# Second half chunk's normalisation two scan slots later, its store one slot later, in groups 1 to 3 of a scan-and-attention kernel

## The chip, the cores and the metric

The kernel runs on one core of one Trainium2 chip. The metric is the device time of one launch in microseconds (us). The figure before is the median of three runs.

## The reference, cut to what matters

The input is 32 sequences of 256 tokens with 256 features, in float32. Each sequence passes through one state-space layer (Mamba-like, with an added conditioning vector), then through two layers of local attention (window 128, 8 heads of 64) and gated feed-forward (hidden size 682), each with its residual. The input is added to the result. In outline, with the layer's names:

```python
xr, gate = split(x @ W_in.T)                # 512 channels each
xc = silu(causal_conv4(xr + cond) + b_conv)
xn = layernorm(xc) * ln_g + ln_b            # over the 512 channels
Bm, Cm, dt = split(xn @ W_xproj.T)          # 16 states each, for each token
Ad = 1 - 0.01 * tanh(dt @ W_dt.T + b_dt) * tanh(A_log)
Bd = Bm * minimum(norm(xn), 1.0)            # the row length of xn, at most 1
for t in range(256):                        # the recurrence; h is (16, 512) for a sequence
    h = clip(h * Ad[t] + Bd[t] * xn[t], -10, 10)
    y[t] = sum(Cm[t] * h)
u = (y + D * xn) * silu(gate) @ W_out.T
for layer in range(2):
    u = u + local_attention(rotary(l2norm(q)), rotary(l2norm(k)), v) @ wo
    u = u + (a * gelu(g)) @ w2 + b2         # a, g from the layernormed u
return x + u
```

So each token's normalised row xn is needed three times: for the figures Bm, Cm, Ad of its token (its length among them), as the input of the recurrence, and in the skip product with D.

## The kernel before, in words

**Tiling.** The sequences are taken in four groups of 8 (`GB`). A group's recurrence runs over 256 steps, in 8 chunks of 32 tokens (`CH`), so there are 32 chunks in all; they are numbered 0 to 31 here, 8 to a group. The state h of a group is one tile of 128 partitions (8 sequences by 16 states) by 512 channels, and one step of the recurrence is one VectorE (DVE) instruction, L716. A chunk has 256 rows (8 sequences by 32 tokens); its layer normalisation is done on two half chunks j = 0 and 1 of 128 rows each (`NJ` = 2).

**Stages.** The scan of group 0 runs alone at first. The scans of groups 1 to 3 then run beside the attention and feed-forward of the groups before them, sequence by sequence (64 units of a sequence and a layer). The attention and feed-forward of the last group end the kernel with no scan beside them.

**What sets the order.** Inside `group_scan`, `at(slot, what, ...)` enters each piece of scan work in a numbered slot; a slot is one step of the recurrence, and the chunk's first step has the number s0. `scan_slots` merges the groups' slots, and the main loop at the end of `program` emits scan slots between the stages of attention and feed-forward. The order of emission is not the final order: a scheduler in the compiler's front end, with costs of its own, takes it as a priority and settles the order of instructions on each engine and the use of the eight PSUM banks. Only a few instructions are pinned with `keep_in_program_order`. Each engine then runs its own instructions in that settled order, and waits at the head of its queue for semaphores.

**The normalisation of half chunk j of a chunk**, with slots counted from s = s0 - 26 + 4j:

- `norm_turn` (slot s): TensorE (PE) transposes xc into a PSUM bank called tp_x.
- `norm_stats` (s + 2): DVE takes mean and variance (L558, L560, L562, L567), and GpSimd (POOL) raises the variance to the power -1/2 (L565).
- `norm_shift` and `norm_apply` (s + 5): ScalarE (ACT) makes the shift (L572) and writes xn from tp_x with scale and shift (L579), which frees the bank.
- `norm_affine` (s + 6): POOL multiplies by the layer's scale and adds its offset (L586, L587).
- `norm_out` (s + 9): SP stores xn in device memory, in xnd (L591), and ACT squares xn with a running sum into ss (L593). The square's own output, sq_x, lies in a ring of two buffers, "th", which the conv's tanh (L504) and the gate's tanh (L768) use too.

**What follows from it.** `length` (slot s0 - 11): DVE clips the sums of squares (L599) and POOL takes the root (L600). `figures` and `figures_in` build each token's figures (DVE L609, PE L618, DVE L630 to L636), and `decays` the decay factors (ACT L643, DVE L648 to L656, POOL L660, L661; L669 makes the read-out matrix ly from them). SP reads each row of xnd back, spread over the 16 states (xrep, L685, slot s0 + t - 6), ACT scales it with beta (L706, s0 + t - 2), and DVE makes the step (L716, s0 + t). PE reads the state out (y, L728), and z is formed (L758 skip product on POOL, L773 gate product and L779, L799 on DVE).

**Other lines that are spoken of.** The conv of the next chunk: L469 and L483 (POOL, start and carry of the conv window), L472 (DVE, conditioning added), L478 (POOL) and L489 (DVE), the taps, L504 (ACT, tanh), L509 (DVE). Projections of later groups are made ahead and loaded with L447; gate inputs are loaded with L455. The attention: L989 (PE, qkv), L1002 (ACT, squares), L1005 to L1019 (DVE) and L1013, L1021, L1022 (POOL, rotary and norm), L1028 (PE, transposes), L1033 (ACT, copies qT and kT), L1215 (PE, scores), L1227 (ACT, exponentials), L1252 and L1271 (PE, row sums and values ov), L1260 (DVE, rinv), L1278 (ACT, oT), L1039 (PE, output). The feed-forward: L1353 (ACT, hT), L1375 (PE, pa), L1386 (ACT, gate ag), L1393 (DVE, gate product ag), L1402 (PE, po_f), L1413 (DVE, residual).

Of the kernel before, what the change touches and what calls it, by code (L numbers as in the profile page):

```python
# [73 lines left out]
def kernel(  # L74
# [147 lines left out]
    def program(ctx, exact):  # L222
# [154 lines left out]
        def group_scan(g):  # L377
# [8 lines left out]
            alone = g == 0  # L386
# [5 lines left out]
            def at(s, what, *args):  # L392
                agendas[-1].setdefault(s, []).append(partial(what, *args))
# [462 lines left out]
            for c in range(NCH):  # L856
                s0 = c * CH
                for hb in range(CH // TB):
                    s = s0 + hb * TB
                    for i in range(NI):  # L860
                        at(s + 4 * i + 5, read_out, c, hb, i)
                    at(s + 21, gated, c, hb)
                    at(s + 25, out_gate, c, hb)
                    at(s + 11, skip, c, hb)
                for ch in range(NC_):
                    at(s0 - 38 + 2 * ch, conv_in, c, ch)
                    at(s0 - 37 + 2 * ch, conv_taps, c, ch)
                    at(s0 - 36 + 2 * ch, conv_th, c, ch)
                    if not alone:
                        at(s0 - 35 + 2 * ch, conv_out, c, ch)  # L870
                for ch, s in enumerate((13, 16, 17, 18)):
                    at(s0 + s + 2, gate_th, c, ch)
                    if not alone:
                        at(s0 + s + 4, gate_out, c, ch)
                at(s0 - 25, raw_copy, c)
                at(s0 - 24, raw_turn, c)
                for j in range(NJ):
                    s = s0 - 26 + 4 * j
                    at(s + 2, norm_stats, c, j)
                    at(s + 5, norm_shift, c, j)  # L880
                    at(s + 5, norm_apply, c, j)
                    at(s + 6, norm_affine, c, j)
                    at(s + 9, norm_out, c, j)
                at(s0 - 11, length, c)
                at(s0 - 9, figures, c)
                at(s0 - 7, figures_in, c)
                at(s0 - 6, decay_th, c)
                at(s0 - 5, decays, c)
                at(s0 - 4, put_c, c, 0)
                at(s0 + 4, put_c, c, 1)  # L890
                for d in range(KM):
                    at(s0 + 45 + 2 * d, copy_y, c, d)
                    at(s0 + 46 + 2 * d, put_y, c, d)
            agendas.append({})
            for c in range(NCH):
# [20 lines left out]
                for hb in range(CH // TB):  # L916
                    s = s0 + hb * TB
# [5 lines left out]
            if alone:  # L923
                n = (NG - 1) * NCH * 2
                for u in range(n):
                    s = -30 + u * (NCH * CH) // n
# [6 lines left out]
        def scan_slots(groups):  # L933


            slots, scans = {}, [group_scan(g) for g in groups]
            for part in range(2):
                for i, agendas in enumerate(scans):
                    for s, what in agendas[part].items():
                        slots.setdefault(i * S + s, []).extend(what)  # L940
            for s in range(min(slots), max(slots) + 1):
                for what in slots.get(s, ()):
                    what()
                yield s
# [717 lines left out]
```

## Time and profile before

| what | value |
|---|---|
| time, median of 3 runs | 3586.82 us (3584.0 to 3589.47) |
| time of the profiled execution | 3582.75 us |
| its span | 3581.0 us |
| mean granted clock | 0.992 |
| PE busy | 3446.0 us, 96% |
| DVE busy | 2667.3 us, 74% |
| ACT busy | 1998.7 us, 56% |
| POOL busy | 1892.2 us, 53% |
| chain that ended last | PE 61%, DVE 19%, DMA 7%, POOL 6%, ACT 4%, issue 3% |
| row scaling L706, 960 times | mean 718 ns |
| recurrence step L716, 1024 times | mean 938 ns |
| gate product L1393, 320 times | mean 474 ns |

The profile records one execution. In lists of waits each line names the engine and instruction that waited, what it waited for, the total, the number of times and the longest. In a timeline each line has start, duration, engine, line, operation, output and input, and in square brackets the engine's idle time just before it with what ended it. Busy time of an engine that is not the latest costs nothing; a wait of PE, which is busy 96% of the span, is the first thing to look for. A chunk of the later groups takes two units, some 103 us (the one followed most closely runs from about 1700 to 1803 us), so one slot is about 3.2 us.

### The profile page before, as it was taken

The numbers are of one execution on the slowest core, as the hardware profiler recorded it, in microseconds if no ns is written. First come the engines' busy times: TensorE is split into PE (matmuls) and PEld (weight loads), VectorE is DVE, ScalarE is ACT, GpSimd is POOL, SyncE is SP. The second block draws the span as 40 slices with busy tenths as digits, with TensorE's granted clock in tenths as the row PEclk, the third lists the DMA queues.
The fourth block names the chain that finished last, engine by engine and source line by source line (L and its number), as shares of the span: only waits on it lengthen the run. The fifth ranks groups of instructions, "written<-read, shape, count | busy, mean of one in ns | idle before, by whom it ended". The sixth has DMA issues, their size and how long they took to land.

```text
span 3581.0 us, 57673 instructions
## 1 busy us (share of the span) xinstructions
PE 3446.0 (96%) x20220; PEld 2253.9 (63%) x20220; DVE 2667.3 (74%) x5049; ACT 1998.7 (56%) x3599; POOL 1892.2 (53%) x1842
## 2 busy tenths in 40 slices
PE   7999989999999999999999999999999999999999
PEld 4555335666656666666666666666666677777777
DVE  5888889888788777888787778888877555555553
ACT  4666656656555665566566655655666444434442
POOL 4433477645556555655565556555544454544551
PEclk9999999999999999999999999999999999999999
DMA  7887665445354545444454555534454112011101
GB/s 207 219 221 213 198 174 149 120 117 143 109 144 125 149 141 148 130 118 127 118 142 125 138 149 140 143 106 131 114 141 122 54 50 61 13 30 38 33 27 37
DMA packets 468767, 435.68 MB, mean 122 GB/s; under 512 B 228723, under 2 KB 308084, under 8 KB 468340
## 3 DMA queue, kind: packets, MB, share of 16 engines
q1 hardware_dynamic: 384018, 419.88, 42.0%
q10 hardware_dynamic: 84450, 12.01, 2.0%
q8 instruction: 163, 2.67, 0.3%
q14 instruction: 136, 1.11, 0.1%
HBM read 383.54 MB, written 46.66 MB: 120 GB/s over the span
## 4 chain that ended last, share of the span: by engine, by line
PE 61%; DVE 19%; DMA 7%; POOL 6%; ACT 4%; issue 3%; SPq 0%; ACTq 0%; DVEq 0%; POOLq 0%
PE ps_qkv L989 13%; PE pa L1375 13%; DVE h L716 7%; PE po_f L1402 7%; DMA xrep<-xnd 5%; PE ps_wo L1039 5%; PE y L728 4%; PE ov L1271 4%; PE sc L1215 3%; PE ps_out L808 3%; PE ps_in L399 2%; PE tr_qk L1028 2%; PE rs L1252 2%; ACT xrep L706 2%; DVE acc L489 2%
## 5 line engine op out<-in xcount | busy, mean ns | idle before, releaser
L716 DVE CUSTOM_DVE_ANT_0 h<-h,xrep,lim 128x512 f32<-128x512 f32 x1024 | 961.0, 938 | 228.9 <-ACT xrep L706 196.6
L706 ACT ACTIVATE xrep<-xrep,beta 128x512 f32<-128x512 f32 x960 | 672.3, 718 | 341.4 <-DMA xrep<-xnd 219.8
L989 PE MATMUL ps_qkv<-qkv,res 128*128 128x512 f32 x1536 | 713.5, 601 | 17.9 <-DVE rinv L1260 8.4
L1375 PE MATMUL pa<-hT,w 128*128 128x256 f32 (+1 forms) x2816 | 675.1, 382 | 11.3 <-DVE zT L799 10.7
L1375 PEld LDWEIGHTS pa<-hT,w 128*128 128x128 f32 (+1 forms) x2816 | 516.9, 188 | 152.9 <-issue 35.4
L1013 POOL TENSOR_TENSOR rot<-rot,swp 128x512 f32<-128x512 f32 x256 | 339.9, 1328 | 475.3 <-DVE swp L1010 423.5
L1021 POOL TENSOR_TENSOR rn<-ss,neg_half 128x8 f32<-128x8 f32 x256 | 466.8, 1823 | 18.4 <-DVE ss L1019 7.8
L989 PEld LDWEIGHTS ps_qkv<-qkv,res 128*128 128x128 f32 x1536 | 282.2, 191 | 301.6 <-issue 241.4
L728 PE MATMUL y<-h,ly 128*32 128x512 f32 x2048 | 348.9, 609 | 16.9 <-DVE h L716 13.9
L1327 POOL TENSOR_TENSOR rstd<-ve,neg_half 128x2 f32<-128x2 f32 x64 | 46.9, 733 | 527.6 <-DVE ve L1325 511.3
L1393 DVE SCALAR_TENSOR_TENSOR ag<-pa,b_sb,ag 128x256 f32<-128x256 f32 x320 | 151.6, 474 | 222.4 <-ACT ag L1386 222.3
L1402 PE MATMUL po_f<-ag,w 128*128 128x256 f32 x1280 | 309.0, 389 | 5.9 <-DVE fo L1413 3.8
L1022 POOL TENSOR_TENSOR rot<-rot,rn 128x512 f32<-128x512 f32 x256 | 289.4, 1130 | 20.0
L1402 PEld LDWEIGHTS po_f<-ag,w 128*128 128x128 f32 x1280 | 236.8, 191 | 71.3 <-issue 12.0
L1386 ACT ACTIVATE ag<-pa,b_sb 128x256 f32<-128x256 f32 x320 | 150.2, 469 | 233.1 <-PE pa L1375 232.1
L1002 ACT ACTIVATE sq<-ps_qkv 128x512 f32<-128x512 f32 x256 | 150.8, 595 | 185.1 <-PE ps_qkv L989 119.4
L1039 PE MATMUL ps_wo<-oT,wo 128*128 128x256 f32 x1024 | 231.7, 379 | 0.5 <-DVE ag L1393 0.5
L489 DVE SCALAR_TENSOR_TENSOR acc<-xr,wc_sb,acc 128x256 f32<-128x256 f32 x384 | 195.1, 531 | 47.7 <-POOL acc L478 47.2
L1005 DVE TENSOR_TENSOR rot<-ps_qkv,rc_sb 128x512 f32<-128x512 f32 x256 | 174.8, 683 | 65.6 <-ACT sq L1002 65.0
L1039 PEld LDWEIGHTS ps_wo<-oT,wo 128*128 128x128 f32 x1024 | 194.4, 190 | 28.1 <-DVE ag L1393 0.9
L1227 ACT ACTIVATE pT<-sc 128x512 f32<-128x512 f32 x384 | 202.3, 603 | 7.6 <-PE sc L1215 5.8
L1271 PE MATMUL ov<-pT,v_sb 128*64 128x256 f32 (+1 forms) x2048 | 183.7, 330 | 19.4 <-DVE ag L1393 19.3
(160 smaller groups left out, 5482.8 us busy)
## 6 DMA issues: line engine op xcount, KB each, us to landing
xrep<-xnd SPq DMA_DIRECT2D x960, 256.0 KB
rb<-inv SPq DMA_DIRECT2D x128, 256.0 KB
xnd<-xn SPq DMA_DIRECT2D x64, 256.0 KB
qkv<-in_wqkv_dram SPq DMA_DIRECT2D x24, 512.0 KB
ahead<-xs_a SPq DMA_DIRECT2D x48, 256.0 KB
xp<-ahead SPq DMA_DIRECT2D x48, 256.0 KB
xd<-xnd SPq DMA_DIRECT2D x192, 64.0 KB
w<-in_w_dram SPq DMA_DIRECT2D x80, 128.0 KB
```

The source lines that it names most:

```text
L489: nc.vector.scalar_tensor_tensor(acc, xr[:, :, k : k + CH], wc_sb[:, ch, k : k + 1], acc, ALU.mult, ALU.add,)
L706: scaled = nc.scalar.activation(bx, ck[c].pop(("bx", t), bx), AF.Copy, scale=ck[c]["beta"][:, t : t + 1])
L716: nc.vector._custom_dve(TENSOR_ADD_SAT, out=h_new, in0=state["h"], in1=bx, s0=ck[c]["lim"][:, 0, t : t + 1], s1=ck[c]["lim"][:, 1, t : t + 1],
L728: nc.tensor.matmul(ck[c]["y", hb][32 * q : 32 * q + 32, :], ly[hb % 2][:, 32 * t : 32 * t + 32], ck[c].pop(("h", hb * TB + t)), start=(i = ...
L989: nc.tensor.matmul(ps, res[b][:, k, t0 : t0 + W], wt["qkv", a][:, k], start=(k == 0), stop=(k == KM - 1),)
L1013: nc.gpsimd.tensor_add(rot, rot, swp)
L1021: nc.gpsimd.tensor_tensor(rn, ss, neg_half, ALU.pow)
L1022: nc.gpsimd.tensor_mul(rot, rot, bc(rn, 2, DH))
L1039: nc.tensor.matmul(po[:, d], wt["wo", 0][:, c, d * P : (d + 1) * P], oT[:, c, :], start=(c == 0), stop=(c == NC_ - 1),)
L1271: nc.tensor.matmul(ov[r * DH : (r + 1) * DH, i, kw * W :], self.qkv[b][2][:, kw, h * DH : (h + 1) * DH], self.p.pop((b, kw, i0 + i, r)), s ...
L1375: nc.tensor.matmul(dst[x], wt["w1", m][:, k, x], self.h[:, k], start=(k == 0), stop=(k == KM - 1),)
L1402: nc.tensor.matmul(self.po[:, d], wt["w2", 0][:, m, d * P : (d + 1) * P], self.ag[m], start=(m == 0), stop=(m == len(MCH) - 1),)
```

## The change

For the second half chunk (j = 1), and only in groups 1 to 3 (`not alone`), shift, apply and the affine step are entered two slots later, and the store with the square one slot later. The first half chunk and group 0 keep their slots. It concerns 24 chunks. No instruction is added, removed or resized. As the changed kernel has one more line, its lines past 880 are numbered one higher than before.

```diff
@@ -877,10 +877,11 @@
                 for j in range(NJ):
                     s = s0 - 26 + 4 * j
                     at(s + 2, norm_stats, c, j)
-                    at(s + 5, norm_shift, c, j)
-                    at(s + 5, norm_apply, c, j)
-                    at(s + 6, norm_affine, c, j)
-                    at(s + 9, norm_out, c, j)
+                    late = 2 if j and not alone else 0
+                    at(s + 5 + late, norm_shift, c, j)
+                    at(s + 5 + late, norm_apply, c, j)
+                    at(s + 6 + late, norm_affine, c, j)
+                    at(s + 9 + late // 2, norm_out, c, j)
                 at(s0 - 11, length, c)
                 at(s0 - 9, figures, c)
                 at(s0 - 7, figures_in, c)
```

## The prediction, made before the changed kernel ran

> **What bounds the kernel now.** I read the stages first. Columns: stretch, its length, then busy us and instruction count of PE, PE's weight loads, DVE, ACT and POOL, then clock and DMA.
>
> ```profile
> 500.00:1400.00 900.00, 858.61 (x5272) 551.09 (x5271) 744.43 (x1389) 541.83 (x988) 522.99 (x501) 0.99 0.48 134
> 1400.00:2700.00 1300.00, 1267.76 (x7907) 842.69 (x7906) 1038.53 (x1974) 782.56 (x1423) 747.14 (x694) 1.00 0.48 131
> 2700.00:3581.00 881.00, 873.17 (x5192) 632.43 (x5191) 471.21 (x921) 375.55 (x643) 400.98 (x332) 1.00 0.16 45
> ```
>
> The changed chunks 8 to 31 lie almost wholly in the first two stretches. There PE is idle for 900 - 858.61 = 41.4 us and 1300 - 1267.76 = 32.2 us. A reordering of other engines can earn only what PE waits: at most 73.6 us, 2.1%, and less if a wait moves. Next, PE's waits in 1400 to 2700 (total, times, longest):
>
> ```profile
> PE ov L1271 <- DVE ag L1393: 15.0, 11, 1.4
> PE ps_qkv L989 <- DVE rinv L1260: 7.1, 12, 0.9
> PE pa L1375 <- DVE zT L799: 6.5, 5, 1.9
> ```
>
> All are on DVE; none is on a normalisation step. ACT's waits from 500 to 2700 tell another story:
>
> ```profile
> ACT stat L572 <- POOL stat L565: 144.9, 40, 8.3
> ```
>
> This looks like the change's target: the shift L572 reaches the head of ACT's queue long before POOL has made its power. The steady chunk around 1700 to 1803 shows why (start, us, engine, operation; idle before it in brackets):
>
> ```profile
> 1716.00 0.47 ACT L1386 ACTIVATE ag<-pa,b_sb 128x256 f32<-128x256 f32 x1 [1.61 <-PE pa L1375]
> 1723.16 0.29 ACT L572 ACTIVATE stat<-nm,stat 128x1 f32<-128x1 f32 x1 [6.69 <-POOL stat L565]
> 1723.49 0.78 ACT L579 ACTIVATE xn<-tp_x,stat 128x512 f32<-128x512 f32 x1
> 1724.17 0.71 ACT L706 ACTIVATE xrep<-xrep,beta 128x512 f32<-128x512 f32 x1
> 1724.78 0.57 ACT L1033 COPY qT<-tr_qk 128x512 f32<-128x512 f32 x1
> 1725.24 0.59 ACT L1033 COPY kT<-tr_qk 128x512 f32<-128x512 f32 x1
> ```
>
> ```profile
> 1717.28 2.09 POOL L1021 TENSOR_TENSOR rn<-ss,neg_half 128x8 f32<-128x8 f32 x1
> 1719.45 1.04 POOL L1022 TENSOR_TENSOR rot<-rot,rn 128x512 f32<-128x512 f32 x1
> 1720.45 1.72 POOL L758 TENSOR_TENSOR xd<-xd,dskip_sb 128x512 f32<-128x512 f32 x1
> 1722.13 0.99 POOL L565 TENSOR_TENSOR stat<-ve,neg_half 128x1 f32<-128x1 f32 x1
> ```
>
> POOL's power stands behind the rotary work and the skip product, so ACT idles 6.69 us. Yet from 1700 to 1752 PE is busy 52.00 of 52.00 us: this stall costs PE nothing. PE waits only later in the chunk, when DVE, almost without a break from 1752 on (26.70 of 28 us up to 1780), is late with its gate product:
>
> ```profile
> 1764.78 0.43 DVE L472 TENSOR_TENSOR xr<-xp,cond_sb 128x256 f32<-128x256 f32 x1
> 1777.61 0.45 DVE L1393 SCALAR_TENSOR_TENSOR ag<-pa,b_sb,ag 128x256 f32<-128x256 f32 x1
> ```
>
> ```profile
> 1778.21 1.52 PE L1271 MATMUL ov<-pT,v_sb 128*64 128x256 f32 x16 [1.37 <-DVE ag L1393]
> ```
>
> **What the Trainium skill says.** "Perfetto Trace Analysis", Sequencer Loop: an engine instruction is put in its engine's queue and waits there for its semaphores. The trace agrees: ACT executed nothing in the 6.69 us although later work was ready. "SBUF — State Buffer", Who interferes with whom: a DVE instruction with two SBUF inputs contends with a GpSimd instruction that reads SBUF. This bears on the scale and offset L586, L587 if they meet other DVE work; the trace has L586 between 1.28 and 1.73 us, in keeping with that, but doesn't show the cause. "ScalarE: Activation LUTs", Rules for kernel authors, asks 2.7 us per switch of table set; here a load takes 1.28 us, so the trace's figure is used.
>
> **The change part by part.** Nothing is added or removed, ACT's 126 table loads included. Slots only set priorities, so I compared the two built programs engine by engine. PE's order is the same throughout.
>
> *Shift and apply (L572, L579), two slots later.* In 22 of 24 chunks L572 keeps the same predecessors in ACT's queue. In the steady chunks (18 to 31) it still stands directly behind the L1386 of 1716.00, and POOL's L565 behind the same rotary work. **The 6.69 us stall stays.** What moves is the next row scaling L706, now behind the copies qT and kT: 1725.72 - 1724.78 = 0.94 us later. A step L716 on DVE is then 0.94 us later, before 1752, where DVE has 52 - 39.28 = 12.7 us of idle time and another L706 is issued some 6 us earlier than now. Value 0; bound without that cover 14 x 0.94 = 13 us, below nothing the 0.94 us that qT and kT come sooner, which PE, busy throughout, can't use: 0. As L579 keeps its place, it frees PSUM bank tp_x no later: 0 in 22 chunks. In chunks 8 and 9 L572 goes behind one or two more row scalings, 0.6 to 1.3 us. The chain through L600 to L609 has about 5 us in hand there by the trace: 0, bounded at -2 to +2 us.
>
> *Scale and offset (L586, L587), two slots later.* They depend on L579 and stay behind it on POOL: 0. If they meet more two-input DVE work, the trace's own spread, 1.73 - 1.28 = 0.45 us, bounds it at ±0.45 us a chunk, hidden before 1752.
>
> *Store and square (L591, L593), one slot later.* On SP the store's first reader is the row load six slots before the chunk's first step; the store moves from 13 slots ahead to 12, leaving 6 slots of about 3.2 us, 19 us: 0. SP also splits or delays gate loads by 4 to 6 row loads; they are used about 50 us later: 0. On ACT the square changes place with the fourth gate tanh in the ring of two "th" buffers, so it now waits for the third gate product L773 (ends 1748.47), and goes behind the four exponentials, to about 1749.8 + 0.6 = 1750.4. The length L599 waits for it on DVE, with the scan step and the convolution queued behind it. Now:
>
> ```profile
> 1744.73 0.61 ACT L593 ACTIVATE sq_x<-xn 128x512 bf16<-128x512 f32 x1
> ```
>
> ```profile
> 1749.12 0.15 DVE L599 TENSOR_SCALAR ss<-ss 128x2 f32<-128x2 f32 x1
> 1751.06 0.81 DVE L716 CUSTOM_DVE_ANT_0 h<-h,xrep,lim 128x512 f32<-128x512 f32 x1 [1.46 <-ACT xrep L706]
> ```
>
> DVE waits for a row until 1751.06 anyway, so 1750.4 is hidden with 0.66 us to spare: 0. Bound: none below, since an earlier finish isn't possible; above, the square's own 0.61 + 0.19 = 0.8 us a chunk.
>
> *What the planner moved along.* In 12 chunks (18 to 29) one L472 goes from ahead of the late L1393 to behind beta (L654). It occupies 1765.12 - 1764.78 = 0.34 us of DVE's queue. PE's wait of 1.37 us behind L1393 shrinks by as much: 12 x 0.34 = **-4.1 us**. It isn't lost at the next wait: before rinv (L1260) DVE idles 2.06 us for an ACT operation that follows PE's own earlier matmuls, and L472 fits there. Only L472's carry copy waits for it on POOL, behind ly (L669). Bounds 0 and -4.1. In chunks 8 to 17 the order is irregular and a few exchanges go either way: value 0, bounded by a fifth of that stretch's 41.4 us, ±8 us.
>
> *Sum.* Profiled execution 3582.75 us (3581.0 span and 1.75 around it) - 4.1 = 3578.65. It lies 4.07 us below the median of the runs, 3586.82; the same step from there gives **3582.7 us**.
>
> **The rivals.**
> *A: it does what it says.* The shift gives way, if only in the irregular chunks, and PE's waits there that come through ACT or the scan disappear: in 500 to 1400 these are y on h 6.9, ps_out on xn 2.8, ps_st on hT 2.8, sc on pT 2.3, tr_qk on oT 1.9 and ps_qkv on oT 1.3, together 18.0 us. For it: one ACT stall, 8.3 us, is followed by a PE wait of 2.8 us on xn. Against: queue positions. 3586.8 - 18.0 = 3568.8.
> *B: slower, the square.* It ends more than 0.66 us later than worked out, past DVE's 1751.06, and the 0.8 us is then passed through DVE's unbroken queue to L1393 and PE in each of 14 steady chunks: 14 x 0.8 = 11.2 us, with the -4.1 swallowed too: 3586.8 + 11.2 = 3598.0. For it: the ring adds a wait on DVE, whose queue is behind ACT's and the reverse. Against: the 1.46 us idle there. It decides from a square ending at 1751.1 in this chunk's time.
> *C: only reshuffling.* L472 earns nothing because L1393 is held by the steps L716 ahead of it: 3586.8. This is the forecast's upper neighbour.
>
> **How the numbers follow.** Forecast 0.45, own range 3575 to 3591 (±8 for chunks 8 to 17); A 0.23; B 0.17; C 0.15. A measurement of this kernel can tell 0.2%, 7.2 us, from no change: faster is below 3579.6, slower above 3594. Faster: A 0.21, forecast 0.15, C 0.03, together 0.39. Slower: B 0.14, forecast 0.02, C 0.02, together 0.18. Same: 0.43. For 8 in 10 the range takes in about half of A and of B: 3568 to 3598.
>
> **What would show it.** Right: in the steady chunks ACT still idles 6 to 7 us before L572 behind POOL's L565 (total near 145 us); PE's wait on L1393 drops from 15 us to about 11; L593 of the second half comes after the exponentials, L599 waits for it briefly, and the next L716 still waits for its row. Wrong: the ACT stall is gone, PE's waits in 500 to 1400 change by more than 8 us, or DVE's wait at L599 exceeds 1.5 us in most chunks.

## The result, and the profile after

The changed kernel takes 3600.18 us (median of 9 runs, 3593.16 to 3608.64), the kernel before 3589.29 us (9 runs, 3584.0 to 3596.06). The ratio is 1.0031, with a 95% interval from 1.0016 to 1.0045: **slower by some 11 us**, where 3582.7 us was forecast and the range ended at 3598. Measured again beside the experiments, the ratio was 1.0035 (1.0021 to 1.0049). The profiled execution took 3608.54 us, with a span of 3606.8 us and a mean granted clock of 0.989. That is 25.8 us over the span before, much more than the medians are apart, so the first task is to see which part of it belongs to the change.

TensorE (PE) runs its instructions in the same order in both programs. So the n-th PE instruction of one trace can be set against the n-th of the other, and the boundary of a stage is the same instruction in all. The table gives the time between four such instructions, those that start at 467.8, 900, 1390 and 2700 us in the first trace of before; it ends with PE's last instruction, some 7 us before the span does.

| trace | to 467.8 | to 900 | to 1390 | to 2700 | to PE's last |
|---|---|---|---|---|---|
| before | 467.8 | 432.3 | 490.0 | 1309.9 | 873.7 |
| before, second trace (experiment 5) | 480.9 | 437.8 | 494.2 | 1313.1 | 873.7 |
| after | 477.7 | 435.1 | 491.4 | 1321.5 | 873.7 |
| after, second trace (experiment 6) | 476.8 | 435.7 | 488.5 | 1322.1 | 873.7 |

The first column varies by 13 us between two traces of the same program; it is no effect of the change. The second and third vary by 4 to 6 us. From 1390 to 2700 us, the steady chunks, the two traces of before are 3.2 us apart and those of after 0.6 us, and the pairs stand **10.3 us** apart: 1321.8 against 1311.5. There the loss lies. It isn't the clock's: from 1390 to 2700 us the granted clock was 1.000 in both traces of after and in the first of before, and 0.997 in the second of before, which is the longer of its pair.

The stages of after, with columns as in the prediction (stretch, length, busy us and count of PE, its weight loads, DVE, ACT and POOL, clock, DMA share, GB/s):

```profile
500.00:1400.00 900.00, 851.76 (x5216) 542.85 (x5216) 739.47 (x1379) 538.01 (x978) 517.58 (x502) 0.99 0.48 132
1400.00:2700.00 1300.00, 1258.30 (x7820) 833.22 (x7820) 1028.91 (x1960) 777.12 (x1418) 744.59 (x694) 1.00 0.47 130
```

PE's idle time from 1400 to 2700 us has grown from 32.2 to 1300 - 1258.30 = 41.7 us. Its waits there (engine, instruction, what it waited for; total, times, longest; lines past 880 are one higher than before):

```profile
PE ov L1272 <- DVE ag L1394: 14.9, 11, 1.4
PE ps_qkv L990 <- DVE rinv L1261: 7.0, 11, 0.9
PE ps_qkv L990 <- DVE ag L1394: 6.9, 10, 0.9
PE pa L1376 <- DVE zT L799: 6.2, 5, 1.8
PE ps_qkv L990 <- DVE xd L779: 4.4, 13, 0.6
```

The wait at ov is what it was (15.0 before). A wait is **new**: qkv for the gate product, 6.9 us in 10 times. The wait of qkv for xd has grown from 2.3 us to 4.4 us.

The stall on ScalarE (ACT) that the change seems made for is still there. First ACT's waits from 500 to 2700 us, then ACT in the chunk that the prediction followed (it now runs 17.9 us later):

```profile
ACT stat L572 <- POOL stat L565: 148.9, 40, 8.4
```

```profile
1733.90 0.47 ACT L1387 ACTIVATE ag<-pa,b_sb 128x256 f32<-128x256 f32 x1 [1.61 <-PE pa L1376]
1741.08 0.30 ACT L572 ACTIVATE stat<-nm,stat 128x1 f32<-128x1 f32 x1 [6.70 <-POOL stat L565]
1741.41 0.78 ACT L579 ACTIVATE xn<-tp_x,stat 128x512 f32<-128x512 f32 x1
1742.09 0.58 ACT L1034 COPY qT<-tr_qk 128x512 f32<-128x512 f32 x1
1742.55 0.60 ACT L1034 COPY kT<-tr_qk 128x512 f32<-128x512 f32 x1
1743.03 0.74 ACT L706 ACTIVATE xrep<-xrep,beta 128x512 f32<-128x512 f32 x1
```

6.70 us against 6.69, behind the same L1387 (L1386 before), and the row scaling behind the copies, as the order of the built program said. The rest of the chunk on DVE (the square's wait, the conditioning add L472 in its new place, and the critical gate products):

```profile
1768.36 0.33 DVE L599 TENSOR_SCALAR ss<-ss 128x2 f32<-128x2 f32 x1 [1.64 <-ACT sq_x L593]
1768.97 0.83 DVE L716 CUSTOM_DVE_ANT_0 h<-h,xrep,lim 128x512 f32<-128x512 f32 x1 [0.29 <-ACT xrep L706]
...
1795.21 0.45 DVE L1394 SCALAR_TENSOR_TENSOR ag<-pa,b_sb,ag 128x256 f32<-128x256 f32 x1
...
1796.66 0.44 DVE L472 TENSOR_TENSOR xr<-xp,cond_sb 128x256 f32<-128x256 f32 x1
1797.02 1.65 DVE L716 CUSTOM_DVE_ANT_0 h<-h,xrep,lim 128x512 f32<-128x512 f32 x2
...
1805.83 0.81 DVE L716 CUSTOM_DVE_ANT_0 h<-h,xrep,lim 128x512 f32<-128x512 f32 x1 [3.21 <-ACT xrep L706]
1806.81 0.81 DVE L716 CUSTOM_DVE_ANT_0 h<-h,xrep,lim 128x512 f32<-128x512 f32 x1 [0.17 <-DVE h L716]
1807.54 0.48 DVE L1394 SCALAR_TENSOR_TENSOR ag<-pa,b_sb,ag 128x256 f32<-128x256 f32 x1
```

And PE:

```profile
1795.81 1.52 PE L1272 MATMUL ov<-pT,v_sb 128*64 128x256 f32 x16 [1.22 <-DVE ag L1394]
1802.67 1.98 PE L990 MATMUL ps_qkv<-qkv,res 128*128 128x512 f32 x4 [0.94 <-DVE rinv L1261]
1808.07 1.98 PE L990 MATMUL ps_qkv<-qkv,res 128*128 128x512 f32 x4 [0.83 <-DVE ag L1394]
```

Read it backwards from PE. At 1808.07 PE waits 0.83 us for a gate product. That stands on DVE behind two steps of the recurrence, and the first of them has waited 3.21 us for its row. Before, the same step waited 2.18 us:

```profile
1787.11 0.81 DVE L716 CUSTOM_DVE_ANT_0 h<-h,xrep,lim 128x512 f32<-128x512 f32 x1 [2.18 <-ACT xrep L706]
```

ACT's scaling of that row waited for its DMA, in before and in after:

```profile
1785.26 0.72 ACT L706 ACTIVATE xrep<-xrep,beta 128x512 f32<-128x512 f32 x1 [2.04 <-DMA xrep<-xnd]
```

```profile
1803.98 0.72 ACT L706 ACTIVATE xrep<-xrep,beta 128x512 f32<-128x512 f32 x1 [3.06 <-DMA xrep<-xnd]
```

Some 1.02 us of additional wait for a row, once in a chunk. Why is the row late? SP's queue in before, then in after:

```profile
1765.23 1.02 SPq L455 DMA_DIRECT2D xg<-in_xT_dram  x2
...
1779.90 1.36 SPq L685 DMA_DIRECT2D xrep<-xnd  x2
```

```profile
1797.13 0.39 SPq L455 DMA_DIRECT2D xg<-in_xT_dram  x1
1797.85 1.37 SPq L685 DMA_DIRECT2D xrep<-xnd  x2
1799.27 0.58 SPq L455 DMA_DIRECT2D xg<-in_xT_dram  x1
```

The gate-input loads L455 take a buffer of the ring that L472 reads from (the tiles xg and xp share its two buffers). With L472 now behind beta, they wait for it until 1797.10 and go out beside the two row loads, not 14 us ahead of them. In this chunk and two others the second load stands behind the rows; in the other 9 chunks both stand ahead of them. What that means for the DMA engines, in the stretches 1778 to 1790 us of before and 1796 to 1808 us of after:

```profile
DMA packets 933, 1.72 MB, mean 143 GB/s; under 512 B 94, under 2 KB 358, under 8 KB 932
```

```profile
DMA packets 2946, 1.85 MB, mean 154 GB/s; under 512 B 2168, under 2 KB 2432, under 8 KB 2946
```

Nearly the same bytes, but three times the packets, 2168 of them under 512 bytes: the gate inputs are gathered in runs of 32 tokens, 128 bytes each.

The chunk followed is no exception. ACT's wait for this one row, found in all 12 chunks, is 1.64 to 2.04 us in before and 2.43 to 3.77 us in after. Its mean over the 12 chunks will be used below; it is 1.82 us in before (1.83 in the second trace) and 2.97 us in after (2.93).

**The theory (T):** the square's new place makes the planner (the compiler's scheduler) put one L472 later in each of 12 chunks; that pushes the gate-input loads to the moment at which two rows are awaited, and delays the two steps behind L472 by 0.36 us (1797.02 - 1796.66), and with them the release of two row buffers. **The rivals:** R1, the late square holds L599 and so DVE's queue (the prediction's rival B); R2, the shift's new neighbours cost a step in each chunk.

### The profile page after: what moved, and what is told of

Same layout as the page of the kernel before. It is cut to its first block, busy times and chain, and to the rows that moved or that the text cites. A ratio compares the mean times of both kernels' runs of the same rounds, so it can differ in the third digit from the quotient of the medians.

```text
span 3606.8 us, 57604 instructions
## 1 busy us (share of the span) xinstructions
PE 3457.0 (96%) x20220; PEld 2260.3 (63%) x20220; DVE 2669.3 (74%) x5049; ACT 1997.2 (55%) x3599; POOL 1887.0 (52%) x1842
## 3 DMA queue, kind: packets, MB, share of 16 engines
q1 hardware_dynamic: 384018, 419.88, 41.7%
## 4 chain that ended last, share of the span: by engine, by line
PE 58%; DVE 20%; DMA 8%; POOL 7%; ACT 4%; issue 3%; SPq 1%; ACTq 0%; DVEq 0%; POOLq 0%
PE pa L1376 12%; PE ps_qkv L990 12%; DVE h L716 8%; PE po_f L1403 6%; DMA xrep<-xnd 6%; PE ps_wo L1040 4%; PE y L728 4%; PE ov L1272 3%; PE sc L1216 2%; PE ps_out L808 2%; PE ps_in L399 2%; PE tr_qk L1029 2%; ACT xrep L706 2%; DVE acc L489 2%; PE rs L1253 2%
## 5 line engine op out<-in xcount | busy, mean ns | idle before, releaser
L716 DVE CUSTOM_DVE_ANT_0 h<-h,xrep,lim 128x512 f32<-128x512 f32 x1024 | 964.2, 942 | 208.8 <-ACT xrep L706 178.2
L1376 PE MATMUL pa<-hT,w 128*128 128x256 f32 (+1 forms) x2816 | 674.9, 382 | 10.2 <-DVE zT L799 8.5
L1328 POOL TENSOR_TENSOR rstd<-ve,neg_half 128x2 f32<-128x2 f32 x64 | 55.2, 862 | 543.5 <-DVE ve L1326 527.1
L1387 ACT ACTIVATE ag<-pa,b_sb 128x256 f32<-128x256 f32 x320 | 150.4, 470 | 233.0 <-PE pa L1376 232.1
```

The lines of the kernel that those rows point to most:

```text
L716: nc.vector._custom_dve(TENSOR_ADD_SAT, out=h_new, in0=state["h"], in1=bx, s0=ck[c]["lim"][:, 0, t : t + 1], s1=ck[c]["lim"][:, 1, t : t + 1],
L1376: nc.tensor.matmul(dst[x], wt["w1", m][:, k, x], self.h[:, k], start=(k == 0), stop=(k == KM - 1),)
```

## The experiments

All edits are against the kernel before, if not said otherwise. In the cuts of code here `late` is 1 for the second half chunk of groups 1 to 3 and 0 elsewhere; "steady stage" is the stretch from 1390 to 2700 us of the table.

**1. Shift, apply and affine alone.**

```diff
-at(s + 5, norm_shift, c, j); at(s + 5, norm_apply, c, j); at(s + 6, norm_affine, c, j)
+at(s + 5 + 2 * late, norm_shift, c, j); at(s + 5 + 2 * late, norm_apply, c, j); at(s + 6 + 2 * late, norm_affine, c, j)
```

> Only shift, apply and affine of the second half chunk two slots later; store and square keep their slot. Theory T (the loss comes from the gate-input loads L455, which in the changed program stand on SP's queue behind a late L472 and between the row loads, 12 chunks of some 0.9 us): this program keeps L472 and L455 where they were before, so 0, between -2 and +3 us against the kernel before. Rival R1 (the late square holds the length L599 on DVE): also 0. Rival R2 (the row scaling behind the copies qT and kT costs a step each chunk): +8 to +13 us.

Measured: 3599.56 us against 3599.86 us for the kernel before on the same chip, ratio 0.9997 (0.9983 to 1.0011). The steady stage takes 1311.9 us, and the mean wait for the row is 1.76 us. Three of the five moved steps do nothing that can be measured; R2 falls.

**2. Store and square alone.**

```diff
-at(s + 9, norm_out, c, j)
+at(s + 9 + late, norm_out, c, j)
```

> Only store and square of the second half chunk one slot later; shift, apply and affine keep their slots. T: L472 and L455 move as in the full change, so +9 to +13 us against the kernel before, and qkv L989 waits on the gate product L1393 some 10 times for 7 us between 1400 and 2700. R1: the same +9 to +13, but with the wait at L599 passed on to PE's wait on L1393 at ov. R2: 0.

Measured: 3604.39 us against 3599.86, ratio 1.0004 (0.9991 to 1.0017). The steady stage takes 1322.7 us, 11.2 us over the mean of before, with qkv waiting on L1393 for 7.2 us in 10 times and a mean wait for the row of 3.04 us, as T says. The total misses the expectation: only a few us are left. From 900 to 1390 us this program takes 487.7 us against 490.0 and 494.2 of before, so a part may be given back there (see experiment 12).

**3. The square alone.** The store and the square are made two entries, and only the square is one slot later.

> Only the square one slot later; the store keeps its slot. T and R1: +9 to +13 us, as the square alone moves L472 and L455 in the planner's order. If the store matters (its rows reach device memory later): 0, and the loss is the store's.

Measured: 3604.38 us against 3599.86, ratio 1.0009 (0.9999 to 1.0019); steady stage 1322.8 us, and 486.6 us from 900 to 1390. The mean wait for the row is 2.99 us. The store plays no part in the steady loss: it comes from **the square's slot**.

**4. The full change with the square two slots later.** This is the cut between T and R1: the square still stands behind the exponentials, but the planner leaves the L472 of T and the L455 loads where they were before (other conv work shifts by a step or two).

```diff
-at(s + 9 + late, norm_out, c, j)              # as in the full change
+at(s + 9 + late, norm_out, c, j, "store"); at(s + 9 + 2 * late, norm_out, c, j, "square")
```

> The full change, but with the square two slots later in place of one. In this program the square still stands behind the four exponentials on ACT, so the length L599 still waits for it, but L472 stands ahead of the late L1393 again and the L455 loads ahead of the skip loads on SP. T: back to the kernel before, -3 to +3 us, and no wait of qkv on L1393 in the steady chunks. R1: +9 us or more, as the square is no earlier. R2: +8 to +13 us.

Measured: 3591.16 us against 3599.86, ratio 0.9974 (0.9961 to 0.9988). By the ratios this is **faster than both kernels**. The steady stage takes 1314.1 us, and the mean wait for the row is 1.87 us. In the chunk followed, DVE waits for the square as in the full change, and then the row comes as in before:

```profile
1755.46 0.30 DVE L599 TENSOR_SCALAR ss<-ss 128x2 f32<-128x2 f32 x1 [1.53 <-ACT sq_x L593]
...
1791.57 0.81 DVE L716 CUSTOM_DVE_ANT_0 h<-h,xrep,lim 128x512 f32<-128x512 f32 x1 [1.97 <-ACT xrep L706]
```

PE's qkv there goes on without a wait, eight in one run where the full change breaks after four:

```profile
1789.65 1.98 PE L989 MATMUL ps_qkv<-qkv,res 128*128 128x512 f32 x4 [0.94 <-DVE rinv L1260]
1791.47 1.03 PE L1375 MATMUL pa<-hT,w 128*106 128x256 f32 x4
1792.33 3.60 PE L989 MATMUL ps_qkv<-qkv,res 128*128 128x512 f32 x8
```

R1 falls as the cause of the 10 us: DVE waits 1.51 to 1.53 us for the square in each of these chunks, against 1.62 to 1.65 us in after, and the loss is gone. The 1314.1 us are 1.6 to 4.2 us over the traces of before and of experiments 1, 8 and 10 that ran at a clock of 1.000, so a small cost of that wait isn't excluded.

**5 and 6. Before and after once more.** The traces are in the table above.

> The kernel before once more, for a second trace. T: against the first trace, PE's sequence runs in step from 1400 to 2700 us (within 2 us), since the loss there belongs to the programs; the start, where group 0's scan is alone, may differ by 5 to 12 us as it did between all the traces so far.

Measured: one time, 3608.49 us, at a granted clock of 0.985. From 1390 to 2700 us it is 3.2 us over the first trace, more than the 2 us expected; the granted clock there was 0.997, not 1.000. The start differs by 13.1 us, also a little more than expected.

> The changed kernel once more, beside the next two. T: +11 to +13 us between 1400 and 2700 against a trace of the kernel before, and a median 9 to 13 us over it. If the first measurement was high by chance: +1 to +5 us, as for the two runs with the square alone late.

Measured: 3607.76 us (5 runs) against 3598.7, ratio 1.0035 (1.0021 to 1.0049); steady stage 1322.1 us. The first measurement wasn't high by chance.

**7 and 8. The gate inputs in long runs**, in the changed kernel and in the kernel before. The bytes are as many, but come from other tokens, so these two kernels' outputs are not the layer's.

```diff
-out=xg[:, k], in_=xT[:, k, b0 : b0 + GB, c * CH : (c + 1) * CH]
+out=xg[:, k].rearrange("p b t -> p (b t)"), in_=xT[:, k, b0 + c]     # groups 1 to 3
```

> The changed kernel, but groups 1 to 3 load the same number of bytes for the gate from other addresses, whose runs are 1 KB long and not 128 bytes: the gates of these groups are computed from other tokens. Order of L472 and L455 as in the changed kernel. If the rows are late because the gate loads' 2048 small packets share the DMA engines with them: the steady chunks' loss falls from 11 us to 5 or less. If they are late because L455 holds SP's queue (0.35 us a row): it stays at 8 or more.

Measured: 3601.23 us against 3598.7, ratio 1.0013 (1.0003 to 1.0023); steady stage 1318.9 us, and qkv waits on L1393 for 4.0 us in 8 times. The loss over the four controls (1311.6 us, the mean of before twice and experiments 8 and 10) falls from 10.2 to 7.3 us, and the mean wait for the row from 2.97 to 2.60 us. That lies between the 5 us or less expected if the small packets were all of it and the 8 us or more expected if SP's queue were.

> The kernel before with the same longer runs for the gate loads of groups 1 to 3 (gates from other tokens), as the control of the last. In the steady chunks the loads lie where no row is waited for: 0 within 2 us from 1400 to 2700; before 1400 the lighter DMA load may gain a few us.

Measured: 3594.68 us against 3598.7, ratio 0.9993 (0.9983 to 1.0003); steady stage 1311.0 us, as expected; mean wait for the row 1.76 us.

**9 and 10. No gate inputs at all**, in the changed kernel and in the kernel before. Groups 1 to 3 leave these loads out, and their gates are computed from other data.

```diff
-for k in range(KM):                     # the two loads of load_x
+for k in range(KM if alone else 0):
-ck[c]["xg"] = xg
+ck[c]["xg"] = xg if alone else w_in_sb[:, :, 0 : GB * CH]
```

> The changed kernel, but groups 1 to 3 load no gate input at all: their gate matmuls read the resident input weights in its place, so gates and output of these groups are computed from other data. L472 stays late in the same 12 chunks; the packets and L455's place on SP are gone. If the late L472, which stands ahead of two steps L716 and so delays the release of two row buffers by some 0.36 us, carries a part of the loss by itself: +3 to +5 us from 1390 to 2700 against the control without gate loads. If only the gate loads matter: 0 to +1.5. The whole loss of 10 us would speak against both.

Measured: 3597.34 us against 3596.88, ratio 1.0000 (0.9988 to 1.0012). The steady stage takes 1315.0 us, 3.4 over the mean of the controls and 2.5 over its own; qkv waits on L1393 for 1.3 us in 4 times. The mean wait for the row is 2.35 us. In the chunk followed the row comes nearly as in before:

```profile
1793.90 0.72 ACT L706 ACTIVATE xrep<-xrep,beta 128x512 f32<-128x512 f32 x1 [2.22 <-DMA xrep<-xnd]
```

> The kernel before without the gate loads of groups 1 to 3 (gates from other data), as the control of the last: 1309 to 1313 us from 1390 to 2700, as the kernel before with its loads, because these lie where no row is waited for.

Measured: 3596.53 us against 3596.88, ratio 1.0003 (0.9992 to 1.0014); steady stage 1312.5 us. The mean wait for the row is 1.86 us. In the kernel before the gate loads cost nothing that can be told. So of the 10 us some 7 go with the loads when they are late, and about 3 stay.

That these 3 belong to the late L472 was not tested by moving it alone, and as a sum they are hardly more than the controls differ among themselves (1309.9 to 1313.1 us). The traces do show what remains. With no gate load on SP's queue, the first of the two row loads still goes out 0.35 us later, against PE's own progress, than in before, in all 12 chunks; that is what L472 takes ahead of the step that frees its buffer. And PE's qkv matmuls, set against the first trace of before, lose 5.7 us in experiment 9, against 0.8 to 1.7 us in experiments 1, 4, 8 and 10 and 11.65 us in after.

**11. The gate loads issued by GpSimd** in the changed kernel.

```diff
-nc.sync.dma_start(                      # load_x
+(nc.sync if alone else nc.gpsimd).dma_start(
```

> The changed kernel with the gate-input loads of groups 1 to 3 issued from GpSimd's queue, not SP's. L472 stays late, and the loads still wait for it and so move their packets at the same moment, but hold no row load on SP. If SP's queue is what makes the rows late: the loss from 1390 to 2700 falls from 10 us to that of the kernel without gate loads. If the packets share the DMA engines with the rows: 8 us or more stay.

Measured: 3607.03 us against 3596.88, ratio 1.0028 (1.0017 to 1.0039); steady stage 1322.2 us, no better than the changed kernel; mean wait for the row 2.85 us. Taking the loads off SP's queue doesn't help. The Trainium skill says as much ("DMA: Bandwidth & Descriptors", Issuing engines are not separate DMA queues): DMAs of every issuing engine run on the same 16 DMA engines; the 1322.2 us agree. Yet the row loads are issued sooner. In after, the first of the two goes out 0.72 to 0.74 us later than in before in 9 of the 12 chunks, where both gate loads stand ahead of it, and 0.35 us later in the other three; here it is 0.35 us in all 12. So the rows are late by what runs beside them more than by SP's queue. It isn't a clean cut, as GpSimd now spends 0.93 us on each load's issue and its own queue is behind.

**12. The square alone two slots later**, with nothing else of the change.

> The kernel before with only the square of the second half chunk two slots later; shift, apply, affine and store keep their slots. Experiment 4, which had these too, was 0.26% faster than the kernel before. If the gain lies in the square's place: 0.1 to 0.4% faster here too, most of it between 900 and 1390 us. If it needs the shift two slots later as well: within 0.1%.

Measured: 3594.85 us against 3596.88, ratio 0.9995 (0.9982 to 1.0009). From 900 to 1390 us it takes 483.1 us, as experiment 4 does with 480.1 us, both well below the 490 to 494 us of before. That the later square gains there isn't shown by this: experiment 11, with the square only one slot later as in after, takes 483.5 us. What sets these three apart from before is also a higher granted clock in that stretch: 0.989 to 0.993, against 0.979 and 0.983 in the two traces of before (in after it is 0.983 and 0.989). Over all 14 traces the stretch is mostly the shorter the higher its clock. Which of the two follows from the other isn't shown. The steady stage takes 1319.9 us here. A wait grows that experiment 4 doesn't have (7.3 us there), though L472 and L455 stand as in before:

```profile
PE pa L1375 <- DVE zT L799: 13.1, 11, 1.9
```

So the square's slot can cost as much by quite another wait, and the gain of experiment 4 needs the shift in its later slot as well, or the chance of how the planner orders the two together; no run tells which.

## Why the prediction was wrong, point by point

Of the 17.5 us between the forecast, 3582.7, and the measured 3600.18, 2.5 us are the start, since the kernel before took 3589.29 us beside it and not 3586.82; 4.1 us are the gain that was counted, and 10.9 us the loss.

**What bounds the kernel.** Right. PE's waits decide, and they come from DVE; the 6.7 us stall of ACT stays and costs nothing. PE is busy throughout in the last stage, 873.7 us in every trace.

**Shift and apply: 0.** Right: experiment 1, ratio 0.9997.

**Scale and offset: 0.** Right, by the same run.

**The square on ACT: 0, with the wait at L599 hidden.** Right in its mechanism and nearly in its size. The square's sum ends at 1768.32, that is 1750.4 in the time of before, as worked out; L599 waits 1.64 us, 19 times for 25.6 us from 500 to 2725 us, and the next step still waits 0.29 us for its row. Rival B did not happen. But one of the prediction's own signs of being wrong, a wait at L599 of more than 1.5 us in most chunks, did show: 1.62 to 1.65 us in 15 of the 24. It was a poor sign, as experiment 4 has 1.51 to 1.53 us in the same 15 chunks and not the loss.

**What the planner moved along: -4.1 us.** In the chunk followed the gain came: PE's lag behind the trace of before goes from 17.91 us to 17.60 us up to ov, 0.31 us where 0.34 was counted. Over the stage it is next to nothing: the instructions concerned (ov L1271 and pa L1375) sum to -0.6 us in both pairs of traces, and PE's wait at ov stayed at 14.9 us where about 11 was forecast. At the next waits of the same chunk the lag grows to 18.69 us.

**The step that failed is the one on SP's queue**: "SP also splits or delays gate loads by 4 to 6 row loads; they are used about 50 us later: 0." It asked who uses the moved transfer, and that was harmless: the gate inputs were never late. It did not ask what the transfer now runs beside. From 1390 to 2700 us PE's qkv matmuls (L989) lose 11.65 us in the first pair of traces and 11.04 us in the second, 6.9 us of it as the new wait for a gate product, behind rows that come about 1 us late in all 12 chunks. So a term valued 0 was worth some +7, by experiment 9.

**A second term was missing.** The prediction let L472 fit into DVE's idle 2.06 us ahead of rinv, and said that only its carry copy waits for it. It does fit there, but it stands in front of two steps L716, whose ends free the row buffers for SP's next loads, and L455 waits for it too. 0.36 us in 12 chunks is 4.3 us; the run without gate loads shows +2.5 to +3.4, and makes L472 the likely cause, without having moved it alone. The two terms, +7 and +3, are the whole of the 10.2 us in the stage by the way they were measured, and the little gain at ov and pa is already in them.

**The irregular chunks: 0, ±8.** The bound held as far as the traces go, and the sign isn't settled. From 900 to 1390 us after takes 491.4 and 488.5 us, before 490.0 and 494.2 us; one trace of a program is good to 4 us there.

**The rival on the slower side** came to nearly the right price (3598.0 us, some 11 us) by luck, for it was placed wrong: the passage from a late row through two steps to a gate product is real, but what is late is the DMA and not the square. **Rival A** didn't happen.

What stays open: why experiment 4 is faster than the kernel before, why the square's slot alone costs less in total (ratio 1.0004 and 1.0009) than the full change, and how the 7 us of the gate loads divide. With the packets in long runs about 3 go; whether the rest is the 512 KB of a chunk's two rows waiting behind 256 KB of any kind wasn't tried.

## What to carry to other kernels

When a planner moves a load, ask not only when its data is used but which transfers it now runs beside, and what waits for those; a load with slack of its own can still delay one that has none. An instruction that fits into idle time can stand ahead of one whose end frees a buffer. And when two programs issue the same instructions on the bound engine, set the traces against each other instruction by instruction: this separated 10 us of effect from 13 us of spread that had nothing to do with it. Put each stage's granted clock beside its length before a gain or a loss there is given a cause.

## What the runs showed of the hardware that was not expected

The start of the kernel, where group 0's scan is alone, took 467.8 us in one trace of before and 480.9 us in another, at mean granted clocks of 0.973 and 0.943 in that stretch, while PE's last 873.7 us, at 1.000, agreed to 0.1 us in all traces. The median of the kernel before was 3589.29 us beside the first result and 3596.88 to 3599.86 us beside the experiments, so each program is compared only with runs of before taken beside it.

256 KB of loads in runs of 128 bytes, put beside two awaited row loads, went with a row that came 1.02 us later in the chunk followed (1.15 us in the mean of the 12 chunks), with the 0.36 us of L472 in it; the mean transfer rate in that stretch rose only from 143 to 154 GB/s.
